# Two bias additions moved from TensorE to VectorE, and four changes of order in the opening and between pairs, in a conditioned MLP block

## The chip, the core and the metric

The kernel runs on one NeuronCore of a Trainium2 chip. The metric is the device time of one execution in microseconds (us). The kernel before took 455.14 us as the median of three runs (454.16 to 455.24). Durations and instants below come from one further execution that was taken with the hardware profiler; instants are counted from the start of its span.

## The reference, cut to what matters

A batch of 32 sequences of 128 tokens, 512 features each, goes through two MLPs that are modulated by a condition vector `t` (32 x 512). Everything is float32.

```python
emb = silu(t) @ ada_w + ada_b                      # 32 x 1536
shift, scale, gate_msa = split(emb, 3)
norm = where(mask, layernorm(x) * (1 + scale) + shift, 0)
fwd  = gelu(norm @ ssm_w1 + ssm_b1) @ ssm_w2 + ssm_b2
bwd  = gelu(norm @ bwd_w1 + bwd_b1) @ bwd_w2 + bwd_b2
x = x + gate_msa * where(mask, fwd + bwd, 0)
ff_ada = silu(t) @ ffada_w + ffada_b               # 32 x 1536
shift_mlp, scale_mlp, gate_mlp = split(ff_ada, 3)
ff_norm = layernorm(x) * (1 + scale_mlp) + shift_mlp
out = x + gate_mlp * (gelu(ff_norm @ ff_w1 + ff_b1) @ ff_w2 + ff_b2)
```

In the text, the "first MLP" is the pair fwd and bwd (its two halves are computed as one MLP with 1024 hidden features), and the "second MLP" is the one with `ff_w1` and `ff_w2`. Only tokens under the mask pass the first MLP; the kernel gathers them into 512 slots, four tiles of 128.

## The kernel before

**The opening, 0 to about 83 us.** The order of all engines is written out by hand here: each engine runs its instructions in the order of the program text, and the program inserts only the semaphores. The conditioning rows are made in three matmul groups: `pm_ss` (shift and scale of the first MLP), `pm_g` (its gate) and `pm_f` (all three kinds of the second MLP). In each, `modulation_bias` (line 296) first puts the bias into the bank with a matmul of four rows, `modulation_matmuls` (309) adds the product with `ada_w` or `ffada_w`, and `modulation_rows` (320) copies the sum out of PSUM with VectorE. The biases lie as four rows in the tile `modb`, and the `1 +` of scale is added to those rows by GpSimd (524).

The four tiles of slots are gathered from `x` by token index (`gather`, 277, on GpSimd's queue). Slots 0 and 1 pass the hidden layer (673 and 204) and the projection `project` (221, weights `w2`, eight blocks of 128 rows in turn); slots 2 and 3 are normalised meanwhile (`statistics`, 158 to 163; `modulated_by_strips`, 347 and 351) and pass the layers later. VectorE also takes the statistics of whole tiles of `x` (`own_statistics`, 171 to 175; each ends with a small power on GpSimd). The projection's banks are seeded by ScalarE (233) with the sum of the biases `b2 + b2b` (792). `finish_slots` (372 to 375) gates the result, takes its statistics and stores it to `x1_wide`, from which GpSimd gathers rows over `raw`, the tiles of `x` (813). VectorE normalises these (842), and side 0 is turned in blocks of 32 x 32 (852), side 1 on TensorE (945).

The matmuls of the second MLP use Strassen-like sums of blocks. `Weights.combine` (394) makes them for `fw1`, the first weight of the second MLP, in four VectorE instructions; `weight_sums` (733) makes further ones, which go to DRAM (737, 738) and are loaded again later (1064).

**Loads.** SyncE's queue holds nearly all loads in program order. The order around the change is: `ada_w` for shift and scale, first half of `w1`, `ada_w` for the gate, second half of `w1`, `raw` 0 and 1, the two biases `b2` and `b2b`, first half of `w2`, `fw1` (2 MB), second half of `w2` (1 MB), `raw` 2 and 3, `ffada_w` in four pieces (3 MB), and then the stores to `x1_wide`, which wait for their data.

**The pairs, from 83 us.** Four pairs of groups of eight tiles each run through the first product (1118) and the second product (1305) of the second MLP. Between two pairs, VectorE prepares the next one: `blocks(side, i)` normalises and turns one tile (929 and 1476), and `to_feature_rows` issues 16 loads of 64 KB (956) that bring the turned blocks into rows of features. The second product needs `first_block`, a sum of hidden blocks (1252), before its step P5, and `seed_and_second_block` (1011, 1012 on ScalarE, 1262 on VectorE) before P6. The order of these steps is again written out by hand, near line 1505.

```python
        second.first_block(1, 2, 4)
        if more_pairs:
            blocks(0, 2)
        second.step(1, late=True)
        now.do(4, "P4")
        if more_pairs:
            blocks(0, 3)
            to_feature_rows(0, nc.sync)
        second.load_gate(1)
        second.first_block(1, 0, 2)
        second.seed_and_second_block(0)
```

Of the kernel before, what the change touches and what calls it, by code (L numbers as in the profile page):

```python
# [9 lines left out]
F32 = mybir.dt.float32  # L10
# [4 lines left out]
ALU = mybir.AluOpType  # L15
# [7 lines left out]
def kernel(  # L23
# [49 lines left out]
    nc = tc.nc  # L73
    B, S, D = x.shape
# [53 lines left out]

    def load_conditioning_bias(at, vec, queue):
        queue.dma_start(modb[at], vec.rearrange("(m j c) -> j m c", m=3, c=P))  # L130

    def load_blocks(t, w):
        nc.sync.dma_start(t, w.rearrange("(k p) f -> p k f", p=P))
# [4 lines left out]

    modb = adap.tile([B + KC, 3, P], F32, name="modb")
    AT_A, AT_F = slice(0, KC), slice(B, B + KC)  # L140
    load_conditioning_bias(AT_A, ada_b, nc.sync)
    n_bias = 2 * KC + HC
# [143 lines left out]
    def x_tile(b, more=0):  # L286
        return xp.tile([P, 2, D + more], F32, tag="x", name=f"x_{b}")

    def gather_slots(token_i):
        both = xp.tile([P, 2, D], F32, tag="x", name=f"xc_{len(xc)}")  # L290
        for c in range(NC // 2):
            gather(both[:, c], token_i[:, c : c + 1])
            xc.append(both[:, c])

    def modulation_bias(pm, at, lo, hi):
        nc.tensor.matmul(
            pm[:, : (hi - lo) * P],
            quarter[at],
            modb[at, lo:hi],
            start=True,  # L300
            stop=True,
            skip_group_check=True,
        )

    def modulation_matmuls(pm, ada, lo, hi, blocks):
        kinds = ada.rearrange("p k (m d) -> p k m d", d=D)
        for k in blocks:
            for j in range(KC):
                nc.tensor.matmul(  # L309
                    pm[ts(j, B), : (hi - lo) * P],  # L310
                    sT[:, k, :],
                    kinds[:, k, lo:hi, ts(j, P)],
                    start=False,
                    stop=True,
                    skip_group_check=True,
                )

    def modulation_rows(pm, mod, lo, hi):
        view = pm[:, : (hi - lo) * P].rearrange("p (m c) -> p m c", c=P)
        nc.vector.tensor_copy(mod[:, lo:hi], view)  # L320

# [200 lines left out]

    def one_more_scale(at):
        nc.gpsimd.tensor_scalar(modb[at, 1], modb[at, 1], 1.0, None, ALU.add)

    one_more_scale(AT_A)

# [41 lines left out]
    nc.scalar.copy(sT.rearrange("p k b -> p (k b)"), ptr[:, : KC * B])  # L569
    quarter = adap.tile([B + KC, P], F32, name="quarter")  # L570
    for at in (AT_A, AT_F):
        nc.scalar.copy(
            quarter[at].rearrange("p (j b) -> p j b", b=B), ident[at, at].unsqueeze(2).to_broadcast([KC, KC, B])
        )
    warm = stp.tile([1, 1], F32, tag="warm", name="warm", bufs=1)
    nc.scalar.activation(warm, s_sb[0:1, 0:1], AF.Gelu)
    for key, vec in (("ssm1", ssm_b1), ("bwd1", bwd_b1), ("ff1", ff_b1)):
# [3 lines left out]
        )  # L581
    load_conditioning_bias(AT_F, ffada_b, nc.scalar)

# [10 lines left out]
    load_behind_gathers(ada_a[:, :, 2 * D :], ada_w[:, 2 * D :])  # L594
    load_blocks(w1[:, :, D:], bwd_w1)
    raw = [x_tile(2 * n, 2) for n in range(2 * G // 2)]
    x_of = {0: [[t[:, :, :D] for t in raw[2 * side : 2 * side + 2]] for side in range(2)]}
# [29 lines left out]

    pm = ps_o.tile([P, 512], F32, tag="o", name="pm_ss")
    modulation_bias(pm, AT_A, 0, 2)
    modulation_matmuls(pm, ada_a, 0, 2, range(KC))  # L630
    slots_of_late = slots_to_count(pick[:, NH:], NC // 2, "s1", (ps_h, "h"))
# [8 lines left out]
    for c in range(2):  # L640
# [4 lines left out]
        if c == 0:  # L645
# [4 lines left out]
            token_i = counted(slots_of_late, slot_col[:, NC // 2 :], NC // 2, "s1", ssm)  # L650
    gather_slots(token_i)
    one_more_scale(AT_F)
    fw1 = fwp.tile([P, KC, FF], F32, name="fw1")
    fw2 = fwp.tile([P, HC, D], F32, name="fw2")
    t_1 = fwp.tile([P, 3, KC // 2, FF // 2], F32, name="t_1")
    t_2 = fwp.tile([P, 3, HC // 2, D // 2], F32, name="t_2")
    fb2 = const.tile([P, D], F32, name="fb2")
    load_blocks(fw1, ff_w1)
    load_blocks(w2[:, KC:], bwd_w2)
    load_raw(2)  # L660
# [31 lines left out]
    pm = ps_o.tile([P, 512], F32, tag="o", name="pm_g")  # L692
    modulation_bias(pm, AT_A, 2, 3)
    modulation_matmuls(pm, ada_a, 2, 3, range(KC))
    modulation_rows(pm, mod1, 2, 3)


# [74 lines left out]
    for f in range(KC):  # L772
        hidden_of_tile(f, 1)
        for done in (f - 1, f) if f % 2 else ():
            t = ssm.tile([P, NH], F32, tag="h", name=f"h_s0_{done}", bufs=HC)
            nc.scalar.activation(t, ph_s[done], AF.Gelu, bias=biasT[:, done : done + 1])
            h1.append(t)
    for n in range(2):
        own_statistics(raw[n], 2, f"x_{n}")
    mv_t, rstd_t = statistics(xc[2:], "s23")  # L780
    strips = of_slots(
        pick, (2, 3), mod1, slice(0, 2), 3 * [(ps_o, "o")] + [(ps_t, "tr")], "part_s2"
    )
    xn_late = []
    for c in range(2):
        xn_late.append(
            modulated_by_strips(
                xc[2 + c], strips, c, spare[1][:, c], mv_t[:, c, 0:1], rstd_t[:, c : c + 1]
            )
        )  # L790
        if c == 0:
            nc.vector.tensor_tensor(b2, b2, b2b, ALU.add)
    h1 += hidden(xT_s, NH, w1, 0, AF.Gelu, "s0", ssm, range(KC, HC))
# [37 lines left out]
    pm = ps_h.tile([P, 512], F32, tag="h", name="pm_f")  # L831
    modulation_bias(pm, AT_F, 0, 3)
    modulation_matmuls(pm, ada_f, 0, 3, range(KC))
# [19 lines left out]

    modulation_rows(pm, mod2, 0, 3)
    normalised_of_side_0(range(2))
# [573 lines left out]
    for p in range(NP):  # L1429
# [32 lines left out]
        if more_pairs:  # L1462
# [4 lines left out]
            def blocks(side, i):  # L1467

                if i == 0:
                    xn[side] = in_turned_blocks(  # L1470
                        group_of_tiles(f"{p + 1}_0")
                        if side == 0
                        else sp.tile([P, G, D], F32, tag="s12", name=f"xn_{p + 1}_1")
                    )
                t = stats[side].normalised(i, xn[side][:, :, i])
                nc.vector.transpose(t, t)
# [30 lines left out]
        second.first_block(1, 2, 4)  # L1507
        if more_pairs:
            blocks(0, 2)
        second.step(1, late=True)  # L1510
        now.do(4, "P4")
        if more_pairs:
            blocks(0, 3)
            to_feature_rows(0, nc.sync)
        second.load_gate(1)
        second.first_block(1, 0, 2)
        second.seed_and_second_block(0)
        fill = {5: [lambda: second.third_block(0)], 7: [lambda: second.third_block(1)]}
# [171 lines left out]
```

## Time and profile before

| What | Value |
|---|---|
| median of three runs | 455.14 us |
| the profiled execution: its own time | 454.21 us |
| its span, first to last instruction | 452.5 us |
| TensorE busy (matmuls) | 445.4 us, 98% of the span |
| VectorE busy | 334.2 us, 74% |
| ScalarE busy | 178.5 us, 39% |
| GpSimd busy | 158.0 us, 35% |
| granted TensorE clock, mean | 1.000 |
| moved by DMA | 70.58 MB, 156 GB/s over the span |

The profiled execution took 1.71 us more than its span (what lies around the first and last instruction), and 0.93 us less than the median of the runs. In the lines of a timeline, the first number is the start in us, the second the length in us; then come engine, source line, operation, and output and inputs by the program's names. Square brackets hold the idle time of the engine before the instruction and what ended it. `PE` is TensorE, `DVE` VectorE, `ACT` ScalarE, `POOL` GpSimd, and `SPq` or `ACTq` a DMA issue on SyncE's or ScalarE's queue. A float32 product of the program shows as two matmul instructions.

### The profile page before, as it was taken

What the parts mean: (1) busy time and instruction counts of PE and PEld (TensorE: products, weight loads), DVE (VectorE), ACT (ScalarE), POOL (GpSimd) and SP (SyncE); (2) the same over time, 40 slices, a digit from 0 to 9 for tenths busy, and PEclk for the clock granted to TensorE, in tenths of its full rate; (3) what the DMA queues carried; (4) which work ended last, traced back from release to release, by engine and by line L of the source; (5) the groups of instructions that cost most, each with busy time, mean ns of one, the idle gap of its engine ahead of it and who ended that gap; (6) DMA issues with size and microseconds to landing.
All of it is one profiled execution on the core that took longest, in us unless ns stands there. A gap on an engine that the chain in (4) does not pass through costs nothing.

```text
span 452.5 us, 6201 instructions
## 1 busy us (share of the span) xinstructions
PE 445.4 (98%) x2151; PEld 370.6 (82%) x2151; DVE 334.2 (74%) x571; ACT 178.5 (39%) x390; POOL 158.0 (35%) x154
## 2 busy tenths in 40 slices
PE   8999999999999999999999999999999999999995
PEld 3885585688888888888888888888888888888884
DVE  5798797877799759987895598868964995434645
ACT  3124127253642551546425524464255144642000
POOL 4220550089770000797700007977000027560000
PEclk9999999999999999999999999999999999999999
DMA  7999449757327817741277177412771434122022
GB/s 254 376 395 408 152 72 332 246 186 236 123 98 159 115 49 257 245 138 36 89 172 112 48 251 245 141 38 90 167 106 58 175 128 129 35 94 93 0 92 98
DMA packets 84916, 70.58 MB, mean 156 GB/s; under 512 B 63368, under 2 KB 63984, under 8 KB 83858
## 3 DMA queue, kind: packets, MB, share of 16 engines
q1 hardware_dynamic: 70066, 58.28, 42.0%
q0 software_dynamic: 4160, 10.54, 6.8%
q10 hardware_dynamic: 10656, 1.33, 2.1%
q8 instruction: 18, 0.29, 0.3%
q14 instruction: 16, 0.13, 0.1%
HBM read 56.46 MB, written 13.70 MB: 155 GB/s over the span
## 4 chain that ended last, share of the span: by engine, by line
PE 94%; DVE 3%; POOL 1%; ACT 1%; issue 1%
PE a_o L1305 22%; PE a_m L1118 20%; PE e_o L1305 18%; PE e_m L1118 15%; PE po_s L221 6%; PE ph_s L204 5%; PE ph_s L673 2%; PE pm_ss L309 1%; PE last L1305 1%; PE a_m_alone L1118 1%; PE pm_f L309 1%; DVE s L1252 1%; PE pl_s L254 1%; PE part_s L333 0%; DVE xn L929 0%
## 5 line engine op out<-in xcount | busy, mean ns | idle before, releaser
L1169 POOL TENSOR_TENSOR ha<-p_m,ha 128x512 f32<-128x512 f32 x20 | 25.8, 1291 | 179.6 <-ACT ha L1176 169.7
L1305 PE MATMUL e_o<-fw,ha 128*128 128x256 f32 x256 | 57.9, 379 | 0.0
L939 ACT ACTIVATE xT<-xT,modT 128x128 f32<-128x128 f32 x112 | 44.2, 480 | 31.8 <-DMA xT<-xn 30.2
L1305 PE MATMUL a_o<-t,hb 128*128 128x256 f32 x240 | 54.1, 379 | 0.0
L1305 PEld LDWEIGHTS e_o<-fw,ha 128*128 128x128 f32 x256 | 48.6, 190 | 6.6
L1305 PEld LDWEIGHTS a_o<-t,hb 128*128 128x128 f32 x240 | 45.6, 190 | 6.2
L1080 ACT ACTIVATE hb<-hb,biasT 128x256 f32<-128x256 f32 x64 | 29.0, 500 | 29.5 <-POOL hb L1202 16.1
L1132 ACT COPY p_m<-e_m 128x512 f32<-128x512 f32 x27 | 15.8, 586 | 48.3 <-PE e_m L1118 44.2
L1305 PE MATMUL e_o<-fw,s 128*128 128x256 f32 x128 | 29.0, 380 | 0.6 <-DVE s L1252 0.6
L885 POOL DMA_INDIRECT x<-x_rows,slot_i x24 | 27.2, 1135 | 6.2 <-issue 5.4
L1169 POOL TENSOR_TENSOR hb<-p_m,hb 128x512 f32<-128x512 f32 x20 | 29.2, 1458 | 0.3
L1305 PE MATMUL a_o<-fw,ha 128*128 128x256 f32 x128 | 28.9, 379 | 0.0
L1305 PE MATMUL a_o<-t,s 128*128 128x256 f32 x128 | 28.9, 379 | 0.0
L221 PE MATMUL po_s<-w,h_s 128*128 128x512 f32 x64 | 28.4, 594 | 0.0
L1176 ACT COPY ha<-e_m 128x512 f32<-128x512 f32 x32 | 18.6, 580 | 24.8 <-PE e_m L1118 20.6
L1305 PEld LDWEIGHTS e_o<-fw,s 128*128 128x128 f32 x128 | 24.2, 190 | 4.3 <-DVE s L1252 1.0
L1305 PEld LDWEIGHTS a_o<-fw,ha 128*128 128x128 f32 x128 | 24.3, 190 | 3.3
L1305 PEld LDWEIGHTS a_o<-t,s 128*128 128x128 f32 x128 | 24.3, 190 | 3.3
L1143 DVE TENSOR_TENSOR e_m<-a_m,ha 128x512 f32<-128x512 f32 x20 | 14.0, 698 | 17.0 <-POOL ha L1169 7.6
L1080 ACT ACTIVATE ha<-e_m,biasT 128x256 f32<-128x256 f32 x48 | 20.1, 469 | 14.4 <-PE e_m L1118 14.2
L1118 PE MATMUL a_m<-xT,tw 128*128 128x256 f32 x96 | 24.7, 380 | 0.0
L1118 PE MATMUL e_m<-s,fw 128*128 128x256 f32 x92 | 23.7, 380 | 0.0
(237 smaller groups left out, 895.0 us busy)
## 6 DMA issues: line engine op xcount, KB each, us to landing
x<-in_x_dram SPq DMA_DIRECT2D x16, 512.0 KB
tw<-t_rows SPq DMA_DIRECT2D x16, 512.0 KB
gate<-gate_rows POOLq DMA_DIRECT2D x8, 1024.0 KB
out_dram<-x SPq DMA_DIRECT2D x15, 512.0 KB
tw<-t_rows SPq DMA_DIRECT2D x16, 384.0 KB
xT<-xn SPq DMA_DIRECT2D x92, 64.0 KB
ada_f<-in_L_cond_ffada_w_dram SPq DMA_DIRECT2D x4, 768.0 KB
ada_a<-in_L_cond_ada_w_dram SPq DMA_DIRECT2D x4, 512.0 KB
```

The source lines that it names most:

```text
L204: nc.tensor.matmul(ph[:, :n], w[:, k, ts(f, P)], xT[:, k, :], start=(k == 0), stop=(k == KC - 1))
L221: nc.tensor.matmul(po, h[f][:, ts(i, P)], w[:, f, :], start=(f == 0 and seeded is None), stop=(f == HC - 1), skip_group_check=seeded is no ...
L309: nc.tensor.matmul(pm[ts(j, B), : (hi - lo) * P], sT[:, k, :], kinds[:, k, lo:hi, ts(j, P)], start=False, stop=True, skip_group_check=True,)
L885: nc.gpsimd.indirect_dma_start(out=xs[i // G][i % G // 2][:, i % 2], out_offset=None, in_=x1_rows, in_offset=bass.IndirectOffsetOnAxis(ap= ...
L939: nc.scalar.activation(out, src, AF.Identity, bias=shift, scale=scale)
L1080: nc.scalar.activation(dst[:, n], src[:, n], AF.Gelu_apprx_tanh, bias=biasT[:, f : f + 1])
L1118: nc.tensor.matmul(bank[:, ts(n, QT)], self.w_block(j, product)[:, ts(n, P)], self.x_block(j, product), start=(product in ("P1", "P5") and ...
L1132: nc.scalar.copy(p5, e)
L1143: nc.vector.tensor_tensor(e, a, p5, add)
L1169: nc.gpsimd.tensor_tensor(self.place(RESULT[j], c), self.p5[j], other, ALU.add)
L1176: nc.scalar.copy(self.place(RESULT[j], c), src)
L1305: nc.tensor.matmul(part, src[:, k, ts(i, P)], w[product][:, k, :], start=(last and k == 0), stop=True, skip_group_check=True,)
```

## The change

Six things change. (1) The bias matmuls of `pm_g` and `pm_f` go; the biases are loaded already spread over the 128 rows (32 batches for each of four blocks), and `modulation_rows` adds them with VectorE, the `1 +` of scale with them. `pm_ss` keeps its matmul. (2) The biases take other loads: one of 64 KB for the gate of the first MLP, on SyncE's queue behind the second half of `w1`; three of 64 KB for the second MLP, behind `ffada_w`; a load on ScalarE's queue, a copy on ScalarE and an addition on GpSimd go. (3) The second half of `w2` is loaded in two halves, one before `fw1` and one behind it. (4) The gather of slot tile 2 is issued ahead of the statistics of slot tile 1. (5) Statistics of slots 2 and 3 are taken tile by tile, each ahead of its own tile; the sum of the biases `b2` and the statistics of `raw[1]` come behind them. (6) Between pairs, `to_feature_rows(0, ...)` comes behind `seed_and_second_block(0)` and issues four of its 16 loads on ScalarE's queue; between the first and the second pair, `blocks(0, 2)` comes later and `first_block(1, 0, 2)` ahead of `blocks(0, 3)`.

```diff
-    def load_conditioning_bias(at, vec, queue):
-        queue.dma_start(modb[at], vec.rearrange("(m j c) -> j m c", m=3, c=P))
+    def load_conditioning_bias(t, vec, kinds):
+        rows = vec.rearrange("(m j c) -> m j c", m=3, c=P)
+        for n, m in enumerate(kinds):
+            nc.sync.dma_start(t[:, n], rows[m].unsqueeze(1).to_broadcast([KC, B, P]))
...
-    modb = adap.tile([B + KC, 3, P], F32, name="modb")
-    AT_A, AT_F = slice(0, KC), slice(B, B + KC)
-    load_conditioning_bias(AT_A, ada_b, nc.sync)
+    modb = adap.tile([P, 3, P], F32, name="modb")
+    nc.sync.dma_start(modb[:KC, :2], ada_b[: 2 * D].rearrange("(m j c) -> j m c", m=2, c=P))
...
-    def modulation_rows(pm, mod, lo, hi):
+    def modulation_rows(pm, mod, lo, hi, bias=None):
         view = pm[:, : (hi - lo) * P].rearrange("p (m c) -> p m c", c=P)
-        nc.vector.tensor_copy(mod[:, lo:hi], view)
+        if bias is None:
+            nc.vector.tensor_copy(mod[:, lo:hi], view)
+            return
+        other = slice(0, hi - lo, 2)
+        nc.vector.tensor_tensor(
+            mod[:, lo:hi][:, other], view[:, other], bias[:, other], ALU.add
+        )
+        if lo <= 1 < hi:
+            nc.vector.scalar_tensor_tensor(
+                mod[:, 1], view[:, 1 - lo], 1.0, bias[:, 1 - lo], ALU.add, ALU.add
+            )
...
-    load_conditioning_bias(AT_F, ffada_b, nc.scalar)
...
     load_blocks(w1[:, :, D:], bwd_w1)
+    load_conditioning_bias(modb[:, 2:], ada_b, (2,))
...
-    gather_slots(token_i)
-    one_more_scale(AT_F)
+            late_slots()
+            gather(xc[2], token_i[:, 0:1])
+    gather(xc[3], token_i[:, 1:2])
...
+    part = KC // 2
+    load_blocks(w2[:, KC : KC + part], bwd_w2[: part * P])
     load_blocks(fw1, ff_w1)
-    load_blocks(w2[:, KC:], bwd_w2)
+    load_blocks(w2[:, KC + part :], bwd_w2[part * P :])
...
-    modulation_bias(pm, AT_A, 2, 3)
     modulation_matmuls(pm, ada_a, 2, 3, range(KC))
-    modulation_rows(pm, mod1, 2, 3)
+    modulation_rows(pm, mod1, 2, 3, modb[:, 2:])
+    load_conditioning_bias(modb, ffada_b, range(3))
...
-    for n in range(2):
-        own_statistics(raw[n], 2, f"x_{n}")
-    mv_t, rstd_t = statistics(xc[2:], "s23")
...
     for c in range(2):
+        if c == 0:
+            own_statistics(raw[0], 2, "x_0")
+        mv, rstd = statistics(xc[2 + c : 3 + c], f"s{2 + c}")
         xn_late.append(
-            modulated_by_strips(
-                xc[2 + c], strips, c, spare[1][:, c], mv_t[:, c, 0:1], rstd_t[:, c : c + 1]
-            )
-        )
-        if c == 0:
-            nc.vector.tensor_tensor(b2, b2, b2b, ALU.add)
+            modulated_by_strips(xc[2 + c], strips, c, spare[1][:, c], mv[:, 0, 0:1], rstd)
+        )
+    nc.vector.tensor_tensor(b2, b2, b2b, ALU.add)
+    own_statistics(raw[1], 2, "x_1")
...
-    modulation_bias(pm, AT_F, 0, 3)
     modulation_matmuls(pm, ada_f, 0, 3, range(KC))
...
-    modulation_rows(pm, mod2, 0, 3)
+    modulation_rows(pm, mod2, 0, 3, modb)
...
         second.first_block(1, 2, 4)
-        if more_pairs:
+        if more_pairs and p:
             blocks(0, 2)
         second.step(1, late=True)
         now.do(4, "P4")
+        if more_pairs and p:
+            blocks(0, 3)
+        second.load_gate(1)
+        if p == 0:
+            blocks(0, 2)
+        second.first_block(1, 0, 2)
+        if p == 0:
+            blocks(0, 3)
+        second.seed_and_second_block(0)
         if more_pairs:
-            blocks(0, 3)
-            to_feature_rows(0, nc.sync)
-        second.load_gate(1)
-        second.first_block(1, 0, 2)
-        second.seed_and_second_block(0)
+            to_feature_rows(0, nc.sync, nc.sync, nc.sync, nc.scalar)
```

More of the change, by code (lines that the diff above doesn't have):

```diff
@@ L287, in x_tile, with late_slots, modulation_bias @@
         return xp.tile([P, 2, D + more], F32, tag="x", name=f"x_{b}")
-    def gather_slots(token_i):
+    def late_slots():
         both = xp.tile([P, 2, D], F32, tag="x", name=f"xc_{len(xc)}")
[L291 to L295, printed above, removed]
+        xc.extend(both[:, c] for c in range(NC // 2))
+    def modulation_bias(pm):
         nc.tensor.matmul(
-            pm[:, : (hi - lo) * P],
-            quarter[at],
-            modb[at, lo:hi],
+            pm[:, : 2 * P],
+            quarter,
+            modb[:KC, :2],
             start=True,
@@ L303, in modulation_bias, with modulation_matmuls @@
         )
-    def modulation_matmuls(pm, ada, lo, hi, blocks):
+    def modulation_matmuls(pm, ada, lo, hi, blocks, begun=False):
         kinds = ada.rearrange("p k (m d) -> p k m d", d=D)
@@ L312, in modulation_matmuls @@
                     kinds[:, k, lo:hi, ts(j, P)],
-                    start=False,
+                    start=(k == 0 and not begun),
                     stop=True,
@@ L521 @@
         )
-    def one_more_scale(at):
-        nc.gpsimd.tensor_scalar(modb[at, 1], modb[at, 1], 1.0, None, ALU.add)
-    one_more_scale(AT_A)
+    nc.gpsimd.tensor_scalar(modb[:KC, 1], modb[:KC, 1], 1.0, None, ALU.add)
     mask_f = adap.tile([B, S], F32, name="mask_f")
@@ L569 @@
     nc.scalar.copy(sT.rearrange("p k b -> p (k b)"), ptr[:, : KC * B])
[L570 to L573, printed above, removed]
-        )
+    quarter = adap.tile([KC, P], F32, name="quarter")
+    nc.scalar.copy(
+        quarter.rearrange("p (j b) -> p j b", b=B), ident[:KC, :KC].unsqueeze(2).to_broadcast([KC, KC, B])
+    )
     warm = stp.tile([1, 1], F32, tag="warm", name="warm", bufs=1)
@@ L628 @@
     pm = ps_o.tile([P, 512], F32, tag="o", name="pm_ss")
-    modulation_bias(pm, AT_A, 0, 2)
-    modulation_matmuls(pm, ada_a, 0, 2, range(KC))
+    modulation_bias(pm)
+    modulation_matmuls(pm, ada_a, 0, 2, range(KC), begun=True)
     slots_of_late = slots_to_count(pick[:, NH:], NC // 2, "s1", (ps_h, "h"))
```

## The prediction

> **What bounds the kernel now.** I read the page's head first, then the waits of TensorE, then its timeline where the change touches it, then VectorE's and SyncE's timelines for what could newly come late.
>
> ```profile
> span 452.5 us, 6201 instructions
> PE 445.4 (98%) x2151; PEld 370.6 (82%) x2151; DVE 334.2 (74%) x571; ACT 178.5 (39%) x390; POOL 158.0 (35%) x154
> ```
>
> ```profile
> PE pm_keep_clock L453 <- DVE zeros L448: 1.3, 1, 1.3
> PE e_o L1305 <- DVE s L1252: 0.6, 1, 0.6
> PE ph_s L673 <- issue: 0.3, 1, 0.3
> PE pl_s L254 <- DVE rank L558: 0.2, 1, 0.2
> ```
>
> TensorE works 445.4 of 452.5 us, and its whole list of waits holds 2.4 us. About 4 us lie behind its last matmul (the final adds and stores). So the time falls only by matmuls that go, or by one of these four waits; and every other edit matters only if it makes TensorE wait anew. The change names two matmul groups (line 296) and the second wait (line 1252).
>
> ```profile
> 20.32 0.48 PE L296 MATMUL pm_g<-modb,quarter 4*128 4x128 f32 x2
> 20.74 1.08 PE L309 MATMUL pm_g<-ada_a,sT 128*32 128x128 f32 x32
> ...
> 49.92 0.91 PE L296 MATMUL pm_f<-modb,quarter 4*128 4x384 f32 x2
> 50.76 2.79 PE L309 MATMUL pm_f<-ada_f,sT 128*32 128x384 f32 x32
> ```
>
> ```profile
> 67.61 0.60 PE L945 MATMUL ptr<-ident,xn 128*128 128x128 f32 x4
> ```
>
> **Gain 1: two bias matmuls.** From start to start they hold TensorE for 20.74 - 20.32 = 0.42 us and 50.76 - 49.92 = 0.84 us, together 1.26 us. No wait stands ahead of them or behind them, so all of it is on the path. [...] The profile shows no gap at other such changes of shape (19.79 to 20.32), so I take 1.26. Clearing the bank by the first product matmul instead of the bias costs nothing: it is a flag.
>
> **Gain 2: the wait at 137 us.**
>
> ```profile
> 132.82 0.65 DVE L1252 TENSOR_TENSOR s<-hb 128x512 f32<-128x512 f32 x1
> 133.39 0.54 DVE L929 TENSOR_SCALAR xn<-x,mv,rstd 128x512 f32<-128x512 f32 x1
> 133.96 0.71 DVE L1476 STREAM_TRANSPOSE xn<-xn 128x512 f32<-128x512 f32 x1
> 134.60 0.65 DVE L1153 TENSOR_TENSOR hb<-a_m,hb 128x512 f32<-128x512 f32 x1
> 135.18 0.53 DVE L929 TENSOR_SCALAR xn<-x,mv,rstd 128x512 f32<-128x512 f32 x1
> 135.74 0.71 DVE L1476 STREAM_TRANSPOSE xn<-xn 128x512 f32<-128x512 f32 x1
> 136.37 0.65 DVE L1252 TENSOR_TENSOR s<-hb 128x512 f32<-128x512 f32 x1
> ```
>
> TensorE reaches P5 of the second half at 136.45 and waits 0.63 us for the sum that starts at 136.37. Two blocks of 1.2 us (929 with 1476) stand between the two sums. In the new order the add of P4 (1153) follows at 133.4, one block fills 134.0 to 135.2, then comes the sum: 135.2 to 135.85, 0.6 us before TensorE asks. Its other input is ScalarE's gelu, which starts behind 1153 and takes 0.91 us: ready at 135.0. So the 0.63 us goes. What is late next is the sum for P6, but that keeps its place in VectorE's order (both blocks still precede it) and is asked for 7 us later. For the other pairs this order is unchanged. Bounds: 0 to 0.63; I take 0.63, because VectorE and ScalarE here follow TensorE's own results and move with it when it runs earlier.
>
> **What comes later: `fw1`.**
>
> ```profile
> 34.77 1.22 DVE L394 TENSOR_TENSOR t<-fw 128x1024 f32<-128x1024 f32 x1 [0.86 <-DMA fw<-in_L_cond_ff_w_dram]
> ...
> 42.36 0.69 DVE L372 TENSOR_TENSOR t_s<-po_s,gs 128x512 f32<-128x512 f32 x1 [0.76 <-PE po_s L221]
> ...
> 54.34 0.55 DVE L842 TENSOR_SCALAR xn<-x 128x512 f32<-128x512 f32 x1 [0.17 <-DMA x<-x_wide,slot_i]
> ...
> 63.53 1.91 DVE L842 TENSOR_SCALAR xn<-x 128x512 f32<-128x512 f32 x4
> ...
> 68.25 1.37 DVE L937 TENSOR_SCALAR xT<-ptr,modT 128x128 f32<-128x128 f32 x4 [0.74 <-PE ptr L945]
> ```
>
> VectorE already waits for `fw1`. DMA runs full there: 394 GB/s from 23 to 35 us. The change puts 512 KB of `w2` and 64 KB of gate bias ahead: 0.52 + 0.07 MB at 394 GB/s is 1.33 + 0.17 = 1.50 us, so the combine starts at 36.27. VectorE was free at 41.60 and waited 0.76 for TensorE; now it is free at 43.10 while TensorE, 0.42 earlier, is done at 41.94. `finish_slots(0)` comes 0.74 us later, and with it the power, the store, the gather and the normalising at 54.34, which hangs on that gather (now 55.08). From there VectorE runs without a gap, so the last normalised tile of side 1 is ready at 63.53 + 1.91 + 0.74 = 66.18. TensorE turns it at 67.61 today, 66.35 after the 1.26: a cover of 0.17 us, against 2.17 now. This is the narrow place of the change. Behind it VectorE waits 0.74 to 0.79 us for each turn, so a lag is caught up within two turns. I take 0; bounds 0 to 0.5 (the three bias loads below, should the store have to queue behind them: 3 x 0.17 us).
>
> **The halves of `w2`.** The first half, asked for at block 4 of `project` (35.11 + 4 x 0.87 = 38.6), now lands before `fw1`; the second, asked for at 40.3, lands about when all of it lands today. No wait before, none after: 0.
>
> **The bias loads.** One of 64 KB ahead of `raw[0]`, three behind `ffada_w` and ahead of the `x1_wide` store. [...] The nearest row here is that store: issued at 45.63, its gather starts at 49.52, so a latency of that order is real in this trace. But loads that are queued overlap it: 394 GB/s was held across many. [...] The conditioning rows need these biases at 52.3 us, after `ffada_w` (DMA is nearly drained from 47): about 4 us of cover. SyncE issues them behind `ffada_w`, some 10 us before the store's data exists. The gate's bias is asked for at about 21.5; `w1` ahead of it is first used at 26.8, and all that waits if it is late is VectorE's counting and statistics, ahead of the idle time before `fw1`. 0.
>
> **The additions on VectorE.** For `pm_g`, 128 columns: 0.29 us as the copy took. For `pm_f`, an add of 256 columns at 0.42 (the `fb_step` row, same shape) and a fused add of 128 at 0.28 (line 347, four in 1.12): 0.70 against 0.56. The extra 0.14 ends at 53.05, before TensorE wants these rows (55.30 - 1.26 = 54.04) and before the gather lands. 0.
>
> **Sums and gathers in the opening.** The same VectorE work, one small instruction more (0.1 us). It ends at about 34.0, ahead of `fw1`. The strips are released at about 31.6 instead of 33.83; TensorE takes their banks at 33.85 today with nothing to spare, 33.43 after, so without this edit Gain 1 would lose 0.4 us there. The sum `b2` ends at 32.2; ScalarE seeds at 33.9. On GpSimd the gather (1.0 us from 16.25) now precedes the power for tile 1, ready about 0.2 us later, just as VectorE asks at 18.18; TensorE wants that tile at 19.79, VectorE finishes at 19.3. 0 in all.
>
> **The turn loads.** They are 19 issues in 13.80 us on SyncE's queue, 0.73 each. [...] Either way only ScalarE waits (7.77 us until 149.79), never TensorE, so the sum gets 0. Price on ScalarE: four issues of 0.61 to 0.73, under 3 us, behind its copies that end at 137.3; its next work waits until 140.84 (3.57 idle; 3.74 between the next two pairs). That work seeds a bank which P2 needs 7 us later. 0.
>
> **Sum.** 1.26 + 0.63 = 1.89 us. The profiled execution would go from 454.21 (span 452.5) to 452.3; that execution lies 0.93 under the median, and the same cut on the median gives 455.14 - 1.89 = 453.25.
>
> **The ways it can go.**
> 1. Both gains arrive: 453.3, with the spread of the runs 452.5 to 453.8. Chance 0.57. For it: every newly delayed step has cover.
> 2. A wait takes the place of the matmuls: side 1's tiles are late at the first turn (line 945), because the cover is only 0.17 us. If `fw1` lands 1 us later than worked out, TensorE waits 0.8: 454.1. Chance 0.24. For it: the thin cover; against it: the queue's rate is well measured.
> 3. The wait at 137 stays, or another engine takes it (gelu behind P4): only 1.26, so 453.9. Chance 0.08.
> 4. Slower: the three bias loads hold up the `x1_wide` store. [...] Against it: queued loads overlap in this trace. Chance 0.11.
>
> Changes under 0.3% (1.37 us) can't be told from none here. Faster than 453.77: nearly all of case 1, a fifth of case 2, a third of case 3, together 0.61. Slower than 456.5: 0.08. The rest, 0.31, within. The range from 452.4 to 455.0 takes in cases 1 to 3 and leaves out case 4.
>
> **What would show it.** Right: no line 296 for `pm_g` and `pm_f`; TensorE's list of waits without line 1252; the first combine near 36.3; `finish_slots(0)` near 43.1; line 945 starting near 66.35 without a wait. Wrong: a wait of TensorE at line 945 on `xn`, a gather from `x1_wide` well after 50.3, or a new wait in the pairs. Most of all, a landing of `fw1` or of that store later than these sums would break it.

## The result, and the profile after

The changed kernel takes 453.42 us (median of 8 runs, 452.42 to 453.58); beside it, on the same chip, the kernel before took 454.82 us (8 runs, 454.16 to 455.24). The ratio is 0.9965, with a 95% interval of 0.9953 to 0.9977. The forecast was 453.3, with a range of 452.4 to 455.0: the number was hit. The working behind it was not right in all its terms, and the profile shows which. The profiled execution of the changed kernel took 453.43 us with a span of 451.7, against 454.21 and 452.5 before: these two differ by 0.8 us, where the sum said 1.89 (the medians differ by 1.40). In both profiled executions the first hidden layer starts at nearly the same instant (16.15 and 16.24 us), so their instants can be compared directly.

First the head of the page of the changed kernel, then the two longest of TensorE's waits; the other two, of 0.3 and 0.2 us, were there before, in the opening.

```profile
span 451.7 us, 6204 instructions
PE 444.0 (98%) x2147; PEld 370.2 (82%) x2147; DVE 334.5 (74%) x573; ACT 177.9 (39%) x389; POOL 158.4 (35%) x154
```

```profile
PE pm_keep_clock L462 <- DVE zeros L457: 1.3, 1, 1.3
PE ptr L950 <- DVE xn L847: 1.1, 1, 1.1
...
```

TensorE's busy time fell by 1.4 us, as the loss of four matmul instructions (0.48 and 0.91 us for the two pairs) demands. The wait at the sum of hidden blocks (line 1252 before) is gone. In its place stands a new wait of 1.1 us at the first turn (line 950; it was line 945 before). TensorE's timeline at the two places, in the changed kernel:

```profile
66.31 0.49 PE L950 MATMUL ptr<-ident,xn 128*128 128x128 f32 x3
67.92 0.33 PE L950 MATMUL ptr<-ident,xn 128*128 128x128 f32 x1 [1.12 <-DVE xn L847]
68.09 1.88 PE L222 MATMUL po_s<-w,h_s 128*128 128x512 f32 x4
...
136.32 1.89 PE L1310 MATMUL e_o<-fw,s 128*128 128x256 f32 x8
```

The projection and the second product's P5 in the kernel before:

```profile
68.05 1.88 PE L221 MATMUL po_s<-w,h_s 128*128 128x512 f32 x4
...
137.08 1.13 PE L1305 MATMUL e_o<-fw,s 128*128 128x256 f32 x4 [0.63 <-DVE s L1252]
```

The first turn begins at 66.31: before, it began at 67.61. So the two matmuls brought 1.30 us, and they had brought it in full by then. But three tiles were turned at once, and the fourth had to wait until 67.92. In the kernel before, the projection behind the turn started at 68.05; now it starts at 68.09. In this execution all of Gain 1 is given back inside one group of four matmuls. What is left is Gain 2: P5 of the second half starts at 136.32, where it started at 137.08, 0.76 us earlier and without a wait.

Why the tile is late can be read backwards from VectorE, and then from GpSimd. VectorE's timeline:

```profile
36.37 1.23 DVE L403 TENSOR_TENSOR t<-fw 128x1024 f32<-128x1024 f32 x1 [1.92 <-DMA fw<-in_L_cond_ff_w_dram]
...
55.14 0.55 DVE L847 TENSOR_SCALAR xn<-x 128x512 f32<-128x512 f32 x1 [2.21 <-DMA x<-x_wide,slot_i]
...
65.85 0.55 DVE L847 TENSOR_SCALAR xn<-x 128x512 f32<-128x512 f32 x1 [0.51 <-DMA x<-x_wide,slot_i]
...
67.32 0.55 DVE L847 TENSOR_SCALAR xn<-x 128x512 f32<-128x512 f32 x1 [0.93 <-DMA x<-x_wide,slot_i]
```

The first two of these lines are where the prediction put them (36.27 and 55.08); the second only by luck. The gather in front of it is 2.43 us late and not 0.74, but from the gather to the normalising it took 3.2 us (51.95 to 55.14) where it had taken 4.8 (49.52 to 54.34). The last two lines are not where the prediction put them: it said that VectorE runs without a gap from 55 us, and that the last tile is ready at 66.18. VectorE waits 0.51 us for the seventh gathered tile and 0.93 us for the eighth. GpSimd's timeline shows what these gathers waited for:

```profile
51.95 1.08 POOL L819 DMA_INDIRECT x<-x_wide,slot_i  x1 [3.33 <-DMA x_wide<-t_s]
...
54.37 0.57 POOL L176 TENSOR_TENSOR t_s<-t_s,half 128x1 f32<-128x1 f32 x1
...
58.77 1.76 POOL L819 DMA_INDIRECT x<-x_wide,slot_i  x1 [1.03 <-DMA x_wide<-t_s]
...
63.43 1.00 POOL L819 DMA_INDIRECT x<-x_wide,slot_i  x1 [0.30 <-issue]
```

The first and the eighth gather in the kernel before, and then the issue of the store that the first one waits for, before and after:

```profile
49.52 1.15 POOL L813 DMA_INDIRECT x<-x_wide,slot_i  x1 [1.65 <-DMA x_wide<-t_s]
...
60.49 1.00 POOL L813 DMA_INDIRECT x<-x_wide,slot_i  x1 [0.30 <-issue]
```

```profile
45.63 0.33 SPq L375 DMA_DIRECT2D x_wide<-t_s  x1
```

```profile
46.39 0.33 SPq L384 DMA_DIRECT2D x_wide<-t_s  x1
```

The first gather from `x1_wide` starts at 51.95; before, at 49.52. The store it waits for was issued at 46.39 (45.63 before), so 1.67 of the 2.43 us of lateness arise between the store's issue and its landing: 5.56 us instead of 3.89. Then comes GpSimd's order: the power of the second store (54.37) stands behind two gathers, although its input was ready at about 52.0; so the second store is issued at 54.97 (52.61 before), the fifth gather waits for it until 58.77 (56.23 before), and the eighth starts at 63.43 (60.49 before).

What holds the first store? The share of busy DMA engines, 40 slices of 47 to 51.5 us, and the packets in that window. First the kernel before, then the changed kernel:

```profile
DMA  7610101000000000000000079999989999999999
...
DMA packets 289, 0.84 MB, mean 186 GB/s; under 512 B 35, under 2 KB 35, under 8 KB 288
```

```profile
DMA  3399999953322223322222110100008999999997
...
DMA packets 623, 0.87 MB, mean 194 GB/s; under 512 B 45, under 2 KB 359, under 8 KB 622
```

Before, the engines are idle from about 48 us until the next stores. Now they stand at two tenths to three tenths of their capacity from 48.0 to 49.5 us, and at one tenth or less until 50.2. In the window 314 packets are between 512 B and 2 KB, where before there was none. These are the bias loads: 3 x 128 rows of 512 B make 384 packets. The rate from 48.0 to 49.5 is 77 to 96 GB/s, not the 394 that I had used. Three loads of 64 KB at about 80 GB/s are 2.5 us.

The trace's records of single packets and of completion signals show how this reaches the store. Each bias load has four signals for its data, where the store has sixteen. I read this as four of the sixteen engines carrying a load; the busy share of 0.30 from 48 to 49 us agrees with that. A packet of 512 B took 29 ns in the median and 27 at the shortest. The first of the four signals comes at 47.71 us for the first load, 48.54 for the second and 49.34 for the third, 0.8 us apart. Of the store's 128 packets, 96 start by 47.96, and the other 32 only from 48.80 to 50.53, among the last bias packets and behind them (the last one starts at 49.88). Of the store's sixteen completion signals, twelve come by 49.06 and the last four from 50.02 to 51.14; before, all sixteen came from 47.65 to 48.74. So a quarter of the store, as much as four of sixteen engines would carry, is late, and with it the gather.

### The profile page after: what moved, and what is told of

The parts are those of the page before. It is cut to its first block, busy times and chain, and to the rows that moved or that the text cites. A ratio compares the mean times of both kernels' runs of the same rounds, so it can differ in the third digit from the quotient of the medians.

```text
span 451.7 us, 6204 instructions
## 1 busy us (share of the span) xinstructions
PE 444.0 (98%) x2147; PEld 370.2 (82%) x2147; DVE 334.5 (74%) x573; ACT 177.9 (39%) x389; POOL 158.4 (35%) x154
## 4 chain that ended last, share of the span: by engine, by line
PE 84%; DMA 8%; DVE 3%; issue 2%; POOL 1%; SPq 0%; POOLq 0%
PE a_o L1310 24%; PE a_m L1123 21%; PE e_o L1310 18%; PE e_m L1123 16%; DMA fw<-in_L_cond_ff_w_dram 3%; PE po_s L222 3%; DMA w<-in_L_cond_bwd_w_dram 3%; DMA x_wide<-t_s 2%; DMA x<-x_wide,slot_i 1%; DVE t L403 1%; PE last L1310 1%; PE a_m_alone L1123 1%; POOL x L819 1%; PE ptr L950 0%; PE pl_s L255 0%
```

## The experiments

Two theories on the lost 1.3 us were stated. **A:** the three bias loads, each on few DMA engines, hold back the landing of the store (A1 is its narrower form: they are slow because only four engines carry them). **B:** `fw1`, which lands later for the half of `w2` ahead of it, makes the whole chain late. Line numbers differ a little from kernel to kernel.

**`w2` whole behind `fw1`, as before.**

```diff
-    load_blocks(w2[:, KC : KC + part], bwd_w2[: part * P])
     load_blocks(fw1, ff_w1)
-    load_blocks(w2[:, KC + part :], bwd_w2[part * P :])
+    load_blocks(w2[:, KC:], bwd_w2)
```

> The changed kernel with the second half of w2 loaded whole behind fw1, as before. Theory A (the three bias loads of 64 KB hold up the store to x1_wide, whatever fw1 does): the combine starts near 35.0 instead of 36.37 us and the store is issued near 45.7, but it still lands near 51.5 behind the bias loads, so the first gather stays near 52, TensorE still waits 0.9 to 1.2 us at the first turn (line 950 of the changed kernel), span 451.5 to 451.8. Theory B (the later fw1 is what makes the turn late): the chain comes 0.7 to 1.4 us earlier, the wait is gone, span near 450.5.

453.29 us (10 runs), ratio to before 0.9975 [0.9965, 0.9986]. The combine starts at 35.19 and the store is issued at 45.78, both earlier; but the first gather starts at 52.16 and the eighth at 63.39, as in the changed kernel. What the store won it spent in the queue: 6.4 us from issue to gather. TensorE still waits 0.7 us at the turn (its opening was 0.6 us later in this execution, which hides as much). So the lateness of `fw1` is not the cause of the late gathers. B falls.

**The three loads on ScalarE's queue.**

```diff
...
-    load_conditioning_bias(modb, ffada_b, range(3))
...
     po_s += [seeded_with_bias(at) for at in (1, 2)]
+    load_conditioning_bias(modb, ffada_b, range(3), nc.scalar)
```

> The changed kernel with its three bias loads of the second MLP issued on ScalarE's queue, behind the seeds of slot tiles 0 to 2 (near 38 us), instead of on SyncE's queue behind ffada_w. Theory A: the store to x1_wide lands near 50, its first gather starts at 50.1 to 50.5 instead of 51.95, the wait of TensorE at the first turn shrinks from 1.1 us to 0 to 0.2, span near 450.5, 1.2 us under the changed kernel. Theory B (fw1 late): the wait stays near 1 us, span near 451.6.

453.55 us (12 runs), 0.9975 [0.9961, 0.9989]. A miss: the first gather came at 52.30, not near 50.3. The opening was 2.3 us late in this execution, so the store too was issued later, at 47.50; from its issue to the gather it took 4.8 us, 0.8 less than in the changed kernel and 0.9 more than before. The wait at the turn isn't in the list, but the late opening alone would hide it. Whether the other queue helps a little stays unclear. It does not take the loads out of the store's way: twelve of the store's completion signals come by 50.04, the last four again later, up to 51.49.

**Two more such loads**, of the same rows into a tile that nothing reads.

```diff
     load_conditioning_bias(modb, ffada_b, range(3))
+    again = adap.tile([P, 2, P], F32, name="again")
+    load_conditioning_bias(again, ffada_b, range(2))
```

> The changed kernel with two more loads of the same 64 KB bias rows behind the three, into a tile that nobody reads. Theory A, about 1 us of queue for each such load: the store lands 2 us later, the wait of TensorE at the first turn grows from 1.1 to about 3 us, span 453.5 to 454. Theory B, or loads that cost only their bytes at 394 GB/s (0.17 us each): the wait grows by 0.3 us, span 452.0.

455.15 us (10 runs), 1.0013 [1.0004, 1.0022]; its span of 453.2 is 1.5 us longer than the changed kernel's. From its GpSimd timeline the first gather, and from TensorE's the turn:

```profile
53.57 1.08 POOL L821 DMA_INDIRECT x<-x_wide,slot_i  x1 [5.03 <-DMA x_wide<-t_s]
```

```profile
69.47 0.33 PE L952 MATMUL ptr<-ident,xn 128*128 128x128 f32 x1 [1.20 <-DVE xn L849]
```

The first gather is 1.62 us later than in the changed kernel, 0.81 us for each added load of 64 KB. Of this, 1.26 us arise because SyncE, still issuing the added loads, issues the store only at 47.65; the store's last signal comes 1.66 us later. So one more load costs 0.81 us, five times the 0.17 us of my sum, and as much as the 0.8 us between the signals of the three loads above. That is less than the 2 us expected, and the listed waits come to 1.5 us, not 3; but the projection behind the turn starts 1.55 us later than in the changed kernel, where the bytes alone would have given 0.3. A holds.

**The bias of `pm_f` on TensorE again**: one load of 6 KB instead of three of 64 KB.

```diff
...
-    load_conditioning_bias(modb, ffada_b, range(3))
+    nc.sync.dma_start(modb[:KC], ffada_b.rearrange("(m j c) -> j m c", m=3, c=P))
...
+    nc.tensor.matmul(pm[:, : 3 * P], quarter, modb[:KC], start=True, stop=True, skip_group_check=True)
-    modulation_matmuls(pm, ada_f, 0, 3, range(KC))
+    modulation_matmuls(pm, ada_f, 0, 3, range(KC), begun=True)
...
```

> The changed kernel with ffada's bias added by a matmul again (one load of 6 KB in place of three of 64 KB; VectorE adds the 1 of the scale). Theory A, the three loads hold back the store's landing by about 2.6 us: the first gather from x1_wide comes some 4 us behind the store's issue, near 50.5 instead of 51.95, the wait of 1.1 us at the first turn goes and 0.84 us of matmul come back: 452.9 to 453.3, some 0.3 us under the changed kernel. Rival G, GpSimd's order alone (the second store's power behind two gathers) makes the tiles late: the first gather moves, the last one stays within 0.4 us of 63.4, the wait stays, and the time is 0.8 us above the changed kernel, 454.2.

452.80 us (12 runs), 0.9966 [0.9955, 0.9978]; span 451.1. The first gather and the turn:

```profile
50.68 1.14 POOL L819 DMA_INDIRECT x<-x_wide,slot_i  x1 [2.05 <-DMA x_wide<-t_s]
```

```profile
67.06 0.60 PE L955 MATMUL ptr<-ident,xn 128*128 128x128 f32 x4
```

The store is issued at 46.39, exactly as in the changed kernel, and its gather starts 1.27 us earlier. The store's sixteen signals come from 48.89 to 49.90, with no four of them apart. All four turns run in one group with no wait. TensorE pays 0.83 us for the matmul again (from 49.37 to 50.20), and the projection behind the turn still starts at 67.50 instead of 68.09. For `pm_f`, the added loads cost about what the removed matmul gains: by the ratio to before, the two kernels are alike (0.9966 and 0.9965).

**The same rows cut by block of 32 rows, all kinds in one load** (four loads in place of three, and four in place of one for the gate).

```diff
-        rows = vec.rearrange("(m j c) -> m j c", m=3, c=P)
-        for n, m in enumerate(kinds):
-            nc.sync.dma_start(t[:, n], rows[m].unsqueeze(1).to_broadcast([KC, B, P]))
+        rows = vec.rearrange("(m j c) -> j m c", m=3, c=P)
+        lo, n = kinds[0], len(kinds)
+        for j in range(KC):
+            row = rows[j : j + 1, lo : lo + n]
+            nc.sync.dma_start(t[ts(j, B), :n], row.to_broadcast([B, n, P]))
```

> The changed kernel with the same bias rows loaded in another cut: one load for each of the four blocks of 32 rows (all its kinds together) instead of one for each kind over all 128 rows; same bytes, same 512-byte pieces, still on SyncE's queue behind ffada_w. Theory A1 (a load whose source has four distinct rows runs on four DMA engines only, 32 pieces of 27 ns on each, 0.9 us a load; the cut by block uses all 16): the DMA share between ffada_w and the store no longer sits at a quarter, the store lands near 50, the first gather starts near 50.3, the wait at the first turn falls from 1.1 us to 0 to 0.2, and from the start of the first hidden layer to the end of the span it takes 434.1 to 434.4 us (435.46 in the changed kernel). Theory A2 (reading the same few rows of DRAM over and over is slow by itself, however it is cut): the wait stays near 1.1 us and that stretch near 435.4.

453.09 us (6 runs), 0.9974 [0.9963, 0.9986]. Each load now has sixteen signals for its data. The store's issue to its gather took 4.3 us instead of 5.56, and no wait of TensorE is listed at the turn. But the gather itself isn't earlier (52.28), because the store was issued only at 47.98; from the first hidden layer to the end it took 434.88 us, more than the 434.1 to 434.4 expected. More small loads held SyncE's queue earlier on (3.75 us for the four of the gate, where one had taken 0.70), and `fw1` came later (issued at 23.61 instead of 21.72, combine at 37.97): a part of the gain went there. With `w2` whole behind `fw1` in addition (both diffs together), which takes out that lateness:

> The same cut by block, and the second half of w2 loaded whole behind fw1 as before. Theory A1: with the store no longer held up, the earlier fw1 gives only more cover at the first turn: no wait there, the same 434.1 to 434.4 us from the first hidden layer to the end. If the lateness of fw1 does cost something by itself, this run is 0.2 to 0.5 us faster than the one with the halves.

452.86 us (5 runs), 0.9956 [0.9943, 0.9969], with no wait of TensorE but the three that were there in the opening before. But from issue to gather it took 5.9 us, and the opening of this execution was 0.7 us late, which hides as much of a wait. So this version was run once more, together with the changed kernel on one chip:

> The changed kernel itself once more, on the chip of the next kernel: 453.2 to 453.6 us if the chip counts for nothing; if chips differ by 0.1%, as the times of the kernel before suggest (454.82 against 454.35 to 454.52), near 453.0. In its trace the wait at the first turn is 1.1 us, less whatever the opening starts later.

453.03 us (6 runs), 0.9966 [0.9954, 0.9978].

> The version with the loads cut by block and the second half of w2 whole behind fw1, beside the changed kernel on one chip. If the cut takes the store's delay away (theory A): no wait at the first turn and 0.5 to 1.0 us under the changed kernel. If it only looked so because that execution opened 0.7 us late: a wait of 0.5 to 0.8 us at the first turn in an execution that opens early, and within 0.3 us of the changed kernel.

453.15 us (6 runs), 0.9967 [0.9955, 0.9979]. The first turns of the two, the changed kernel first:

```profile
66.26 0.49 PE L950 MATMUL ptr<-ident,xn 128*128 128x128 f32 x3
67.29 0.33 PE L950 MATMUL ptr<-ident,xn 128*128 128x128 f32 x1 [0.54 <-DVE xn L847]
```

```profile
66.53 0.60 PE L951 MATMUL ptr<-ident,xn 128*128 128x128 f32 x4
```

Both executions opened early (first hidden layer at 16.18 and 16.30), and the version cut by block doesn't wait at the turn: its first gather starts at 51.18, its eighth at 61.99, 0.8 us ahead of the changed kernel's (52.04 and 62.79). But its store is also issued 0.9 us earlier (45.59 and 46.48), and from issue to gather both take 5.6 us; two of the store's signals still come late, at 50.05 and 50.38. So the cut doesn't take the store's delay away. It only shortens it: with `w2` whole and the loads uncut it was 6.4 us, with the cut 5.6 and 5.9. Neither edit alone brings the first gather forward (52.28 and 52.16); both together do. In these two executions the version cut by block is 0.6 us shorter (spans 450.5 and 451.1). In the medians nothing of that can be seen. And the changed kernel itself waits only 0.5 us here, with the same instants up to the first gather: what it gives back of Gain 1 differs from one execution to the next.

**GpSimd's order**: the first two gathers behind the second store's power; the loads stay.

```diff
-    for i in range(2):
-        take_first_rows(i)
     store_rows.append(finish_slots(1, project(1, h1, w2, "s1", seeded=po_s[1]), gs[1]))
-    for i in range(2, 2 * G):
+    for i in range(2 * G):
         take_first_rows(i)
```

> The changed kernel with the first two gathers of side 0 issued behind the second store's power on GpSimd; nothing of the loads changes. If GpSimd's order is part of the chain: the second store is issued near 52.7 instead of 54.97, no gather waits for it, the eighth gather starts near 62.2 instead of 63.43, the wait at the first turn falls from 1.1 to under 0.2 us, and the time to 452.2 to 452.6. If the landing of the first store alone counts: the eighth gather stays at 63.4 or comes later by the 0.6 us that the first gathers lose, and the time is 453.4 to 454.0.

452.79 us (6 runs), 0.9959 [0.9945, 0.9972]. The second store is issued at 52.59, no gather waits for it, and the eighth starts at 62.50. The wait at the turn is gone; a smaller one took its place. From the list of TensorE's waits, and from ScalarE's timeline:

```profile
PE ph_s L205 <- ACT h_s L209: 0.7, 1, 0.7
```

```profile
63.32 1.39 ACTq L959 DMA_DIRECT2D xT<-xn  x2
64.76 0.47 ACT L209 ACTIVATE h_s<-ph_s,biasT 128x256 f32<-128x256 f32 x1 [4.82 <-DVE t L741]
```

The first tiles of side 0 are gathered 0.9 us later, so their turn loads, two of which are issued by ScalarE, start at 63.32 (62.11 in the changed kernel), and the gelu behind them in ScalarE's order starts at 64.76 (63.55). TensorE waits 0.7 us for its bank. The projection behind the turn starts at 67.66 (68.09 in the changed kernel). So GpSimd's order is a link of the chain, beside the loads.

**The order between the pairs alone**: the kernel before with only part (6) of the change.

> The kernel before with only the new order between pairs and the four turn loads on ScalarE's queue. My account of the changed kernel says that its whole net gain in the profiled execution is this part: the wait at line 1252 is gone and the span is 0.7 to 0.8 us shorter than before, 451.7; the rival account, that both parts of the change still contribute about half of what arrived, gives 0.4 us, span 452.1.

453.57 us (10 runs, 453.38 to 455.67), 0.9989 [0.9976, 1.0001]. The wait at 137 us is gone. Its profiled execution opened 1.9 us late, so I count from the start of the first hidden layer to the end of the span: 435.42 us, against 436.35 before and 435.46 in the changed kernel. In these executions part (6) alone gives all of the net gain. The medians don't settle it: this kernel lies 0.82 us under the kernel before (454.39), the changed kernel 1.40 under its own.

**All turn loads of side 0 on SyncE's queue.** Tried first on the version cut by block, then on the changed kernel itself.

```diff
-            to_feature_rows(0, nc.sync, nc.sync, nc.sync, nc.scalar)
+            to_feature_rows(0, nc.sync)
```

> The cut by block, with all 16 turn loads of side 0 on SyncE's queue, as before. My account: the four loads on ScalarE's queue change nothing on TensorE's path, so the time is that of the cut by block within 0.1 us (434.1 to 434.4 from the first hidden layer to the end). The rival, that they buy time between the pairs, gives a new wait of TensorE or 0.3 us and more.

454.07 us (12 runs), 0.9992 [0.9979, 1.0006], against 453.09 for the same kernel with four loads on ScalarE. This I had not expected. The median alone says little here: six runs lie at 452.93 to 453.40 and six at 454.74 to 455.67. But the profiled execution, one of the first six, takes 384.15 us from the start of the projection behind the first turn to the end of the span, against 383.57 with four loads on ScalarE, in small gaps in pair 1.

> The changed kernel with all sixteen turn loads of side 0 on SyncE's queue. If the queue does nothing for the time (my sum): within 0.2 us of the changed kernel, 453.3 to 453.6. If late turns leave gaps between TensorE's matmuls at the start of pair 1, as the pair of runs with the loads by block suggested: 0.5 us more, 453.9 to 454.1, with ScalarE's first scale of pair 1 later than 149.2 and matmul groups that take 0.1 to 0.2 us more between 177 and 187 us.

454.34 us (12 runs), 0.9994 [0.9984, 1.0003]: not to be told from the kernel before, and its interval lies above that of the changed kernel (0.9953 to 0.9977). From the start of the projection to the end it takes 384.67 us, the changed kernel 383.61 and the kernel before 384.45. ScalarE's first scaling for pair 1 and VectorE's first sum behind it, in the changed kernel:

```profile
149.22 0.49 ACT L944 ACTIVATE xT<-xT,modT 128x128 f32<-128x128 f32 x1 [6.50 <-DMA xT<-xn]
```

```profile
164.16 1.23 DVE L991 TENSOR_TENSOR s<-xT 128x1024 f32<-128x1024 f32 x1 [5.50 <-ACT xT L944]
```

The same two, and then TensorE, with all loads on SyncE:

```profile
151.03 0.49 ACT L944 ACTIVATE xT<-xT,modT 128x128 f32<-128x128 f32 x1 [10.03 <-DMA xT<-xn]
```

```profile
165.74 1.23 DVE L991 TENSOR_TENSOR s<-xT 128x1024 f32<-128x1024 f32 x1 [7.24 <-ACT xT L944]
```

```profile
178.82 1.03 PE L1123 MATMUL a_m<-xT,fw 128*128 128x256 f32 x4
179.93 1.13 PE L1123 MATMUL e_m<-s,fw 128*128 128x256 f32 x4
```

The turn loads wait for the last of four turned tiles. In the new order that tile (line 1481) comes behind the sum of hidden blocks and ends 0.64 us later than before. With 16 loads on one queue the first scaling is then 1.8 us later than with four of them on ScalarE. ScalarE hands that on to VectorE (165.74 instead of 164.16), and VectorE has no idle time from there to 181 us, when it empties TensorE's banks (line 1148 at 179.18 instead of 177.61). TensorE is held back in small steps: groups that follow each other at 0.86 us stand 1.11 us apart at 178.82. Between 173 and 187 us these steps come to about 1.2 us, none large enough to stand in the list of waits.

## Why the prediction was right, and where it was wrong

**Gain 2** was right: 0.76 us from start to start against 0.63. The sum of hidden blocks starts at 135.24, as worked out (135.2).

**Gain 1** arrived in its size (1.30 against 1.26) and was given back at the first turn, all or in part (1.3 us from start to start in one execution; in the other one the wait was 0.5). That is case 2 of the prediction, at the place it named as narrow, and near its size of 0.8 us, but not by its cause: `fw1` was on time to 0.1 us. The cause is that of case 4, the bias loads ahead of the store, which from its issue to its gather took 1.67 us more. That the first product matmul clears the bank cost nothing: the two product groups take 1.08 and 2.79 us in both kernels.

**The failed term is the bound of 3 x 0.17 us for the three bias loads.** I took 64 KB at the queue's rate of 394 GB/s, 0.17 us each; the two added loads show 0.81 us each. The rate was measured on other loads, and these have four data signals each, where the store has sixteen. Their source has four blocks; cut by block, each load had sixteen signals. What sets the number is not shown. For case 4 too, with its chance of 0.11 and the 0.08 for a time above 456.5 us, no run shows a delay that long: the signals of the three loads are 0.8 us apart, so they follow each other with their data; from the store's issue to its gather it took 1.67 us more; and with five such loads the time was 455.15 us. Three loads at 0.8 us are 2.4 us. Set in the place of the 0.5 us of the bound, they make the lateness at the turn 0.74 + 2.4 = 3.1 us against a cover of 0.91 (2.17 - 1.26), a wait of up to 2.2 us by this estimate, where the two executions show 1.1 and 0.5. I had the slot for it in the sum, and left it at 0.

**"From there VectorE runs without a gap" failed** for the same reason and one more: the last tiles hang on the second store, which GpSimd's order ties to the first. The experiment with the power ahead of the gathers shows that link.

**"The turn loads: 0" failed** as a price for the edit. I reasoned that only ScalarE waits for them. It is so in the kernel before, but the new order of the pairs makes the last turned tile 0.64 us later and TensorE 0.8 us earlier, and with that the cover is gone: without the four loads on ScalarE's queue, Gain 2 is lost again. Their own price was off too, though nothing waits for it: the four issues hold ScalarE for 4.37 us, not under 3, and its next work starts at 141.53 instead of 140.84. The sum of part (6) was right only because both of its edits were made together.

**Right at 0:** the halves of `w2` (0.9975 with `w2` whole, 0.9965 in halves, with intervals that overlap), the additions on VectorE (0.42 + 0.28 us, and nothing waits), the order of the opening's statistics and gathers. Only the first of them was tried alone; for the others the trace shows no more than that no wait stands there.

**The number itself** owes something to luck. The medians of the two kernels differ by 1.40 us on one chip and by 1.50 on another, so the sum of 1.89 was 0.4 to 0.5 us too large, and 1.1 us by the profiled executions. But it was taken from 455.14 us, the median of three runs, and with more runs the kernel before stands at 454.82, and at 454.35 to 454.53 on the chips of the experiments.

**No version is shown to beat the changed kernel.** The one cut by block with `w2` whole (0.9956 and 0.9967), the one with GpSimd's order changed (0.9959) and the one with the bias of `pm_f` on TensorE (0.9966) all lie within the interval of the changed kernel (0.9965 and 0.9966).

**How much of Gain 1 stayed** can be read from six executions that opened within 0.2 us of one another. From the start of the first hidden layer to the start of the projection behind the first turn, the kernel before takes 51.90 us; the changed kernel 51.85 and 51.28; the version with the bias of `pm_f` on TensorE 51.35; the one with GpSimd's order changed 51.56; and the one cut by block with `w2` whole 50.67. So the last one keeps 1.23 of the 1.26 us, and the changed kernel nearly nothing or half. From the projection to the end, the kernel before takes 384.45 us and all these versions 383.53 to 383.64: Gain 2 is there each time.

**Open:** how much of Gain 1 the changed kernel keeps on average. In its two executions the first gather started at 51.95 and 52.04; the difference came from what lies behind it (the eighth at 63.43 and 62.79), with one gather that took 1.76 us in the first and 1.11 in the second. Open too is why with the loads cut by block two of the store's signals still come late (50.05 and 50.38).

## What to carry to other kernels

Cost a load by a measured load of its own form, and not by the rate of the queue it stands in: here a broadcast of four blocks to 128 rows cost 0.81 us, where its bytes at that rate suggested 0.17, and the store behind three of them took 1.67 us longer to its gather. When a wait is removed by putting one instruction ahead of another, follow the displaced one to its last user, also when a slack of many microseconds seems to lie between. A gain on TensorE shortens every cover that was measured against it; re-read each cover after the subtraction, with GpSimd's and ScalarE's program order in it.

## What the runs showed of the hardware that was not expected

Loads of 64 KB from four blocks, broadcast to 128 rows, ran at some 80 GB/s (77 to 96 from 48.0 to 49.5 us), a fifth of the 394 GB/s of the loads from 23 to 35 us in the kernel before. Of the store behind them, twelve of sixteen completion signals came by 49.06 us and the last four only from 50.02 to 51.14.

TensorE's opening differs between the profiled executions. The thirteen matmuls of one group (`part_s`, from about 12 us) took 1.02 us in the profiled executions of before and after, 1.26 to 1.91 us in five others, and the first hidden layer started between 15.56 and 18.56 us, at mean granted clocks of 0.997 to 1.000. What follows the loads does not always move with it: where the hidden layer started 2.3 us late (the loads on ScalarE's queue), the first combine came 0.2 us later than in the changed kernel and the first gather 0.35 us; where it started 1.9 us late (part (6) alone), the combine came 1.0 us later than in the kernel before and the gather 2.3. So in the first of these two the late opening can hide a wait on DMA at 67 us.
